# The up-products of a group: two blocks of rows in turns, one product each

## The chip, the cores and the metric

The kernel runs on one core of one Trainium2 chip. The metric is the time of one execution on the device in microseconds (us). The core has five engines that work side by side, each through its own queue in order: TensorE (PE, matrix products; PEld are its loads of the stationary operand), VectorE (DVE), ScalarE (ACT), GpSimd (POOL), and SyncE (SP), which here only issues DMAs. Products are written to PSUM, which holds few tiles; DVE and ACT read it, POOL and the DMAs do not use it here.

## The reference

The input x is (2, 4096, 256). A gated recurrence runs over the 4096 steps of each sequence, then a feed-forward part with binary weights; each has a residual and a layer norm behind it:

```python
u = x @ W_in + b_in
g = sigmoid(x @ W_gate + b_gate)
h_t = tanh(h_{t-1} @ A + u_t @ Bm)          # 64 states, step by step
y_t = g_t * (h_t @ C.T + u_t @ D.T) + (1 - g_t) * x_t
x = layernorm(x + (y @ W_out + b_out + x))
# bw = mean(|w|, axis=1) * sign(w), for w1 and w2
h = gelu(x @ bw1.T + b1)                    # 256 -> 1024
x = layernorm(x + (h @ bw2.T + b2))         # 1024 -> 256
```

All values are float32.

## The kernel before

**Chunks.** Each sequence is cut into 64 segments of 64 steps, and all 128 segments (both sequences) run side by side, so that a recurrence step is one product and one tanh on 128 columns (`steps`, L156 to 158). The 8192 tokens are worked in 16 chunks of 512. The first 85 us load data, form u and most of the gates, and run the first steps. Then a loop over the chunks c follows (L718 to 783), which interleaves pieces of several chunks, and into which `emit` strews the remaining recurrence steps: a piece is a generator, and at each of its `yield`s a counter of PE time may let one step be put in.

**A chunk's pieces.** `mix` (L365, products ps_y at L370) and `mix_end` form y with DVE's operations d (L377, L382) and tg (L385); `project` (L388, products ps_z at L395) multiplies by W_out in two halves, DVE adds the residual (L406) and gathers statistics (L256, L260, L265), POOL takes the power -1/2 (L266). `shift` (nm, L271) and `norm` (L279, four ACT operations for most chunks) apply the layer norm. `turn` (L418) transposes the result (ps_t, L423); ACT copies it to fp32r as xhi (L431), and DVE takes the rest, xlo (L433). `rest` adds a row on POOL (L355).

**The feed-forward part.** The 1024 hidden rows are 8 blocks of 128, worked in four groups g of two. `up(g)` (L442) makes, for each block, four products of 512 columns into a PSUM tile ps_h (L451): sign weights times xhi for both halves of the 256 features, then times xlo. GELU on ACT (L458) reads the tile and writes h; after both blocks ACT copies h to fp32r, hhi (L467). `low(g)` (L470) has DVE compute hlo = h - hhi (L474). `down(g)` (L532) multiplies hhi and hlo by the second sign weights, 32 products of 256 columns into ps_o (L490), 16 after each half of the group. After the fourth group `scale` (o, L506) and `add` (L512) move the sum out on DVE, and `store` norms it (L281) and stores it.

**Order.** The engines' orders are written out by hand: PE, ACT, DVE and POOL execute what the code emits, in that order. In chunk c it is: up 0, low 0, down 2 of chunk c-1, shift and norm of c+1, mix of c+2, up 1, down 3 of c-1, add and statistics of c-1, one gate (c from 1 to 12), turn of c+1, low 1, rest, up 2, low 2, store of c-1, down 0, first half of the projection of c+2, up 3, down 1, low 3, second half of the projection. A group is written c.g below: 13.0 is group 0 of chunk 13. In the first loop pass (c = 0) and for the last chunk there is less to put between: up 1 of chunk 0 follows up 0 at once, and up 2 of chunk 15 follows up 1 at once (L772 to L776). The last chunk ends with `down_end` (L544), which finishes block by block of tokens; its group 3 copies hi and subtracts lo in two halves (`apart`).

**PSUM tiles.** The pool p_1 (tag h) has three tiles of one bank, taken in turn by ps_h, ps_g and ps_u. p_m (tag m) is a single tile of two banks, taken in turn by ps_y, ps_t and ps_z. p_2 (tag o) is the single ps_o. A product that is first to write a tile waits until the last reader of the tile's earlier use is done. In SBUF h has two buffers, hhi and hlo three.

Of the kernel before, what the change touches and what calls it, by code (L numbers as in the profile page):

```python
# [8 lines left out]
FP = mybir.dt.float32  # L9
# [7 lines left out]
P = 128  # L17
B, T, DM, S, H = 2, 4096, 256, 64, 1024
KD = DM // P
# [4 lines left out]
N = 512  # L24
# [13 lines left out]
def gated_recurrence_then_binary_ffn(  # L38
# [24 lines left out]
    p_1 = ctx.enter_context(tc.tile_pool(name="p_1", bufs=3, space=PSUM))  # L63
# [15 lines left out]
    sg1 = cp.tile([P, KD, H], FR, name="sg1")  # L79
# [249 lines left out]
    class Chunk:  # L329
# [112 lines left out]
        def up(self, g, apart=False):  # L442
            nm = f"{self.nm}_{g}"
            h = wk.tile([P, 2, N], FP, tag="h", name=f"h{nm}")
            hi = wk.tile([P, 2, N], FR, tag="hhi", name=f"hhi{nm}", bufs=3)
            self.h[g] = h, hi
            for i in range(2):
                j = 2 * g + i
                ps = p_1.tile([P, N], FP, tag="h", name=f"ps_h{nm}_{i}")
                for n, (k, part) in enumerate((k, p) for p in (self.hi, self.lo) for k in range(KD)):  # L450
                    nc.tensor.matmul(  # L451
                        ps,
                        sg1[:, k, bass.ts(j, P)],
                        part[:, k, :],
                        start=n == 0,
                        stop=n == 2 * KD - 1,
                    )
                nc.scalar.activation(  # L458
                    h[:, i, :],
                    ps,  # L460
                    AF.Gelu,
                    bias=b1_c[:, j : j + 1],
                    scale=al1[:, j : j + 1],
                )
                if i == 1:
                    for part in range(2) if apart else [slice(0, 2)]:
                        nc.scalar.copy(hi[:, part, :], h[:, part, :])  # L467
                yield
# [379 lines left out]
```

## Time and profile before

| | |
|---|---|
| median of three runs | 453.91 us (452.56 to 455.10) |
| profiled execution | 452.42 us, span from first to last instruction 450.6 us |
| PE busy | 439.4 us, 98% of the span; granted clock 0.996 in the mean |
| DVE, ACT, POOL busy | 358.7, 261.2, 173.6 us |
| L451, products ps_h | 512: 256 with xhi, 256 with xlo |
| L458, GELU | 128, 776 ns each in the mean |
| L467, copy to hhi | 65, 1037 ns |
| L474, hlo | 65, 1314 ns |

How to read it: a row of the profile names the line, the engine, the operation, out<-in by the program's tile names, the shape and a count. In the rows ordered by time the first number is the start in us from the span's start, the second the time from there to the end, of several merged instructions where the count is over 1; in square brackets stands the idle time of the engine before it and what ended it. Rows of waits read: who <- whom: us in total, times, longest. An fp32 product is recorded as two instructions. The end of a matmul is modelled, so that products overlap in the records; their starts are what tells the pace. PEclk gives the granted clock of TensorE in tenths, a digit for each fortieth of the span.

### The profile page before, as it was taken

What the parts mean: (1) busy time and instruction counts of PE and PEld (TensorE: products, weight loads), DVE (VectorE), ACT (ScalarE), POOL (GpSimd) and SP (SyncE); (2) the same over time, 40 slices, a digit from 0 to 9 for tenths busy, and PEclk for the clock granted to TensorE, in tenths of its full rate; (3) what the DMA queues carried; (4) which work ended last, traced back from release to release, by engine and by line L of the source; (5) the groups of instructions that cost most, each with busy time, mean ns of one, the idle gap of its engine ahead of it and who ended that gap; (6) DMA issues with size and microseconds to landing.
All of it is one profiled execution on the core that took longest, in us unless ns stands there. A gap on an engine that the chain in (4) does not pass through costs nothing.

```text
span 450.6 us, 6727 instructions
## 1 busy us (share of the span) xinstructions
PE 439.4 (98%) x2506; PEld 357.2 (79%) x2506; DVE 358.7 (80%) x597; ACT 261.2 (58%) x424; POOL 173.6 (39%) x177
## 2 busy tenths in 40 slices
PE   9999999999999999999999999999999999999992
PEld 5665766788888888888978787979798888897982
DVE  0245937967989798989898988898998989887774
ACT  2443541585656575847574747475666656565871
POOL 1001400644545434343454454535353545433413
PEclk9999999999999999999999999999999999999998
DMA  8898824220223222322233122212111020201012
GB/s 298 306 318 289 291 64 135 69 85 0 71 95 116 96 70 95 116 95 70 95 97 112 49 71 93 73 45 72 47 51 67 13 93 1 93 1 48 1 47 99
DMA packets 14837, 44.50 MB, mean 99 GB/s; under 512 B 2000, under 2 KB 3024, under 8 KB 14800
## 3 DMA queue, kind: packets, MB, share of 16 engines
q1 hardware_dynamic: 14224, 43.65, 28.8%
q8 instruction: 21, 0.34, 0.3%
q10 hardware_dynamic: 576, 0.37, 0.3%
q14 instruction: 16, 0.13, 0.1%
HBM read 31.43 MB, written 8.39 MB: 88 GB/s over the span
## 4 chain that ended last, share of the span: by engine, by line
PE 88%; DVE 6%; ACT 2%; DMA 2%; POOL 1%; issue 0%; POOLq 0%; DVEq 0%
PE ps_h L451 24%; PE ps_o L490 23%; PE ps_z L395 12%; PE ps_g L313 11%; PE ps_y L370 6%; PE ps_s L157 5%; PE ps_u L131 4%; PE ps_t L423 3%; DVE hlo L474 1%; DMA xt<-in_xT 1%; ACT xn L279 1%; DVE xn L281 1%; PE ps_s L154 1%; ACT h L458 1%; DVE bs_a L256 1%; ACT hhi L467 1%
## 5 line engine op out<-in xcount | busy, mean ns | idle before, releaser
L458 ACT ACTIVATE h<-ps_h,bias_c,al 128x512 f32<-128x512 f32 x128 | 97.5, 776 | 77.4 <-PE ps_h L451 72.2
L490 PE MATMUL ps_o<-sg,hhi 128*128 128x256 f32 x496 | 120.3, 282 | 0.0
L490 PE MATMUL ps_o<-sg,hlo 128*128 128x256 f32 x496 | 119.0, 279 | 0.1
L474 DVE TENSOR_TENSOR hlo<-h,hhi 128x1024 fp32r<-128x1024 f32 (+1 forms) x65 | 84.2, 1314 | 23.6 <-ACT hhi L467 23.6
L490 PEld LDWEIGHTS ps_o<-sg,hhi 128*128 128x128 f32 x496 | 93.6, 189 | 2.3
L490 PEld LDWEIGHTS ps_o<-sg,hlo 128*128 128x128 f32 x496 | 93.4, 188 | 2.5 <-DVE hlo L474 0.3
L451 PE MATMUL ps_h<-xhi,sg 128*128 128x512 f32 x256 | 92.3, 441 | 0.0
L451 PE MATMUL ps_h<-xlo,sg 128*128 128x512 f32 x256 | 80.2, 394 | 0.2
L355 POOL TENSOR_TENSOR xn<-xn,bo_r 128x256 f32<-128x256 f32 x64 | 60.7, 979 | 45.5 <-DMA xn<-in_x 45.5
L355 POOL TENSOR_TENSOR xn<-xn,b_r 128x256 f32<-128x256 f32 x64 | 71.5, 1145 | 1.2 <-PE ps_t L423 1.2
L467 ACT CAST hhi<-h 128x1024 fp32r<-128x1024 f32 (+1 forms) x65 | 67.3, 1037 | 2.0
L313 PE MATMUL ps_g<-xt,w_gate 128*128 128x384 f32 (+3 forms) x208 | 67.1, 432 | 0.2 <-DMA xt<-in_xT 0.2
L266 POOL TENSOR_TENSOR rs_a<-rs_a,neg_half 128x4 f32<-128x4 f32 x16 | 17.2, 1075 | 122.3 <-DVE rs_a L265 104.6
L158 ACT ACTIVATE st<-ps_s 64x128 f32<-64x128 f32 x112 | 30.1, 269 | 56.2 <-PE ps_s L157 55.8
L395 PE MATMUL ps_z<-w_out,tg 128*128 128x256 f32 x256 | 61.2, 380 | 0.0
L451 PEld LDWEIGHTS ps_h<-xlo,sg 128*128 128x128 f32 x256 | 48.1, 188 | 11.9 <-DVE xlo L433 0.9
L451 PEld LDWEIGHTS ps_h<-xhi,sg 128*128 128x128 f32 x256 | 46.1, 189 | 12.8 <-issue 6.2
L266 POOL TENSOR_TENSOR rs_b<-rs_b,neg_half 128x4 f32<-128x4 f32 (+1 forms) x17 | 19.2, 1132 | 95.5 <-DVE rs_b L265 84.3
L157 PEld LDWEIGHTS ps_s<-st,wab 128*128 128x128 f32 x224 | 37.5, 189 | 22.8 <-ACT st L158 9.5
L395 PEld LDWEIGHTS ps_z<-w_out,tg 128*128 128x128 f32 x256 | 45.9, 190 | 5.0
L279 ACT ACTIVATE xn<-xn,nm_a,rs_a 128x256 f32<-128x256 f32 x60 | 31.2, 591 | 26.5 <-DVE nm_a L271 26.5
L157 PE MATMUL ps_s<-st,wab 128*128 128x128 f32 x224 | 43.9, 277 | 0.0
(73 smaller groups left out, 485.3 us busy)
## 6 DMA issues: line engine op xcount, KB each, us to landing
xt<-in_xT SPq DMA_DIRECT2D x35, 512.0 KB, 4.6
xn<-in_x SPq DMA_DIRECT2D x16, 512.0 KB, 3.5
out_y<-xn SPq DMA_DIRECT2D x15, 512.0 KB, 2.6
hu<-st SPq DMA_DIRECT2D x32, 128.0 KB, 2.9
w1t<-in_w1T SPq DMA_DIRECT2D x2, 512.0 KB, 5.7
w1n<-in_w SPq DMA_DIRECT2D x2, 512.0 KB, 6.6
w2t<-in_w2T SPq DMA_DIRECT2D x2, 512.0 KB, 4.7
xt<-in_xT SPq DMA_DIRECT2D x2, 256.0 KB, 3.5
```

The costliest lines, as they stand in the source:

```text
L157: nc.tensor.matmul(p_h, ab, st[:, j].rearrange("p b k -> p (b k)"), start=True, stop=True)
L158: nc.scalar.activation(h_of[:, j + 1].rearrange("p b k -> p (b k)"), p_h[TOP, :], AF.Tanh)
L266: nc.gpsimd.tensor_tensor(rs, rs, neg_half[:, cut], ALU.pow)
L279: nc.scalar.activation(r, r, AF.Identity, bias=self.sh[:, i : i + 1], scale=rs)
L313: nc.tensor.matmul(ps[:, cut], w_gate[:, k, bass.ts(m, P)], xt_[:, k, cut], start=k == 0 and i == 0, stop=k == KD - 1, skip_group_check=True,)
L355: nc.gpsimd.tensor_tensor(r[:, i, :], r[:, i, :], row, ALU.add)
L395: nc.tensor.matmul(self.ps_z[:, i, :], self.y[:, k, bass.ts(i, P)], w_out[:, k, :], start=k == 0, stop=k == KD - 1,)
L451: nc.tensor.matmul(ps, sg1[:, k, bass.ts(j, P)], part[:, k, :], start=n == 0, stop=n == 2 * KD - 1,)
L458: nc.scalar.activation(h[:, i, :], ps, AF.Gelu, bias=b1_c[:, j : j + 1], scale=al1[:, j : j + 1],)
L467: nc.scalar.copy(hi[:, part, :], h[:, part, :])
L474: nc.vector.tensor_sub(lo[:, i, :], h[:, i, :], hi[:, i, :].bitcast(FP))
L490: nc.tensor.matmul(ps[:, i, :], part[:, j % 2, bass.ts(tb, P)], sg2[:, j, :], start=j == 0 and part is self.h[j // 2][0] and first, stop=j ...
```

## The change

Only `up` is changed. Both PSUM tiles are taken at its start. The loop over the four products (feature half and part) is now the outer one, and the loop over the two blocks the inner one, so that the products go: first product of block 0, first of block 1, second of block 0, and so on. The two GELUs, the copy after the second one and the two `yield`s follow behind all eight products. `low`, `down` and the order of the pieces stay as they were.

```diff
-            for i in range(2):
-                j = 2 * g + i
-                ps = p_1.tile([P, N], FP, tag="h", name=f"ps_h{nm}_{i}")
-                for n, (k, part) in enumerate((k, p) for p in (self.hi, self.lo) for k in range(KD)):
+            both = [p_1.tile([P, N], FP, tag="h", name=f"ps_h{nm}_{i}") for i in range(2)]
+            for n, (k, part) in enumerate((k, p) for p in (self.hi, self.lo) for k in range(KD)):
+                for i in range(2):
                     nc.tensor.matmul(
-                        ps,
-                        sg1[:, k, bass.ts(j, P)],
+                        both[i],
+                        sg1[:, k, bass.ts(2 * g + i, P)],
                         part[:, k, :],
                         start=n == 0,
                         stop=n == 2 * KD - 1,
                     )
+            for i in range(2):
+                j = 2 * g + i
                 nc.scalar.activation(
                     h[:, i, :],
-                    ps,
+                    both[i],
                     AF.Gelu,
                     bias=b1_c[:, j : j + 1],
                     scale=al1[:, j : j + 1],
```

## The prediction

> **What bounds the kernel now.** I read the page's busy shares first, then its slices, the waits, and last the order of time in one chunk.
>
> ```profile
> PE 439.4 (98%) x2506; PEld 357.2 (79%) x2506; DVE 358.7 (80%) x597; ACT 261.2 (58%) x424; POOL 173.6 (39%) x177
> ...
> PEclk9999999999999999999999999999999999999998
> ```
>
> TensorE (PE) is busy in every slice until the last and its clock is full. Between 97 and 413 us its start times show hardly a hole. So time can be won only by quicker products, and lost wherever PE starts to wait. The waits say how near it is to that:
>
> ```profile
> ACT h L458 <- PE ps_h L451: 72.2, 40, 2.8
> ...
> DVE hlo L474 <- ACT hhi L467: 23.6, 29, 3.5
> ...
> PEld ps_h L451 <- DVE xlo L433: 0.9, 2, 0.5
> ...
> PE ps_t L423 <- ACT xn L279: 0.9, 4, 0.4
> ```
>
> ScalarE (ACT) waits 40 times for up-products, VectorE (DVE) waits 29 times for ACT's hi copy. PE's matmuls themselves wait only under 1 us a line once the chunks run. One chunk shows the loop that runs through all three:
>
> ```profile
> 222.81 1.69 ACT L458 ACTIVATE h<-ps_h,bias_c,al 128x512 f32<-128x512 f32 x2 [0.66 <-PE ps_h L451]
> ...
> 224.53 1.05 ACT L467 CAST hhi<-h 128x1024 fp32r<-128x1024 f32 x1
> ...
> 225.61 1.23 DVE L474 TENSOR_TENSOR hlo<-h,hhi 128x1024 fp32r<-128x1024 f32 x1 [0.81 <-ACT hhi L467]
> ...
> 231.53 1.21 DVE L506 TENSOR_TENSOR o<-ps_o,al_r 128x1024 f32<-128x1024 f32 x1
> ...
> 235.83 1.22 DVE L433 TENSOR_TENSOR xlo<-ps_t,xhi 128x1024 fp32r<-128x1024 f32 x1
> ...
> 237.46 1.60 PEld L395 LDWEIGHTS ps_z<-w_out,tg 128*128 128x128 f32 x8
> ```
>
> Products of group 0 end, GELU twice, hi copy, and DVE, which stood idle 0.81 us for that copy, starts hlo. From there DVE works its queue without a hole (nm, d twice, tg, o, xn, statistics) until xlo ends at 237.05. xlo is the last reader of the single p_m tile, and the projection that takes this tile loads its first weights at 237.46. That is 0.41 us, or 0.36 after the 0.05 us a release takes (in chunk 0 xlo ended at 96.65 and PE's load started at 96.70). What comes later than 0.36 us stops PE.
>
> **The change part by part.**
>
> *Instructions.* None is added or removed: 512 products with 512 weight loads, 128 GELUs, 65 hi copies and as many lo subtractions. No DMA and no SP or POOL instruction is moved. A recurrence step that fell between the two blocks of a group now comes behind all eight products; its two small products cost the same 0.22 us there.
>
> *Pace of the products.* They now change bank at each product, not once in four. In the trace the step from product 4 to 5 of a group is that bank change: 231 ns from start to start, beside 230 to 233 ns for the other steps. So 0, with bounds of ±3 ns × 512 = ±1.5 us. [...] The fp32 projection products do run at 216 here, these do not. [...] But this trace holds four idles within 413.1 to 415.3 us, PE busy only 3.11 of 4.00 us, and a granted clock of 1.00 there; the idles expected below are shorter. So 0.
>
> *GELU and what follows.* Block 0 used to end after product 4, so that its GELU ran under products 5 to 8. Now it ends with product 7. The two ways stand in the trace: where ACT waited for products (the first line), the pair takes 1.69 us; where both blocks were ready, it takes less:
>
> ```profile
> 418.40 1.45 ACT L458 ACTIVATE h<-ps_h,bias_c,al 128x512 f32<-128x512 f32 x2
> 419.88 1.05 ACT L467 CAST hhi<-h 128x1024 fp32r<-128x1024 f32 x1
> ```
>
> A GELU starts 0.44 us after the start of its last product (429.81 to 430.25 below). Before, the copy starts 0.44 + 0.81 us after the start of product 8. Now the first GELU starts 0.44 us after product 7 starts, the copy 1.48 us later (418.40 to 419.88), and product 8 starts 0.23 us after product 7: 0.44 + 1.48 − 0.23 = 1.69 against 1.25. So the hi copy is late by 0.44 us wherever ACT stood idle for the group. Groups 1 are excepted: their GELUs wait for the norm anyway.
>
> *Where that lands.* The direct consumers, the down products, have hlo 2.7 us or more ahead of need from chunk 1 to 13: no cost. But hlo of group 0 starts DVE's unbroken run, and behind it queue nm (so the norm on ACT), d, tg, o, xn, the statistics and xlo, for which the projection's load waits. In half of the chunks d itself waits some 0.1 us for ps_y (once 0.57), which absorbs as much. The room before the load, read as above for projections 3 to 14, is 0.27, 0.51, 0.33, 0.28, 0.14, 0.36, 0.27, 0.47, 0.33, 0.28, 0.15 and 0.00 us; the lateness that reaches xlo is 0.44, 0.39, 0.35, 0.33, 0.33, 0.44, 0.44, 0, 0.36, 0.33, 0.33, 0.44. What exceeds the room is 0.17 + 0 + 0.02 + 0.05 + 0.19 + 0.08 + 0.17 + 0 + 0.03 + 0.05 + 0.18 + 0.44 = **1.38 us**. PE's stall moves the next group too, so it recurs in each chunk. Bounds: 0, if DVE makes it good, and 3.7 us, if in about half of the chunks one DVE operation more falls under POOL traffic (L385 takes 1.65 us instead of 1.22 beside POOL's additions), which removes the room.
>
> *The norm of the last chunk.* From hlo of 13.0 at 388.90 to the norm at 413.10 DVE, ACT and POOL form one chain, and the transposes wait for that norm (the 0.9 us of the waits). Late by 0.44: **+0.44 us**; 0 to 0.9.
>
> *First group.* Up 0 of chunk 0 waits for the low half of x before products 3 and 4 (0.9 us of holes), with four hi products now ahead of it: it ends at 89.19 instead of 89.98, −0.79. But up 1 follows at once, and here the third buffer matters: a group's second tile is the previous group's first. Up 1 needs it at its second product (89.42), while its GELU, started at 89.16, frees it at about 89.90: +0.48. Its late copy of x for projection 2 costs another 0.04. Together **−0.27 us**; −0.8 to +0.2.
>
> *Last chunk.* Up 2 follows up 1 at once, too:
>
> ```profile
> 430.25 0.78 ACT L458 ACTIVATE h<-ps_h,bias_c,al 128x512 f32<-128x512 f32 x1 [2.85 <-PE ps_h L451]
> 431.19 0.78 ACT L458 ACTIVATE h<-ps_h,bias_c,al 128x512 f32<-128x512 f32 x1 [0.15 <-PE ps_h L451]
> ```
>
> Up 1 runs 429.12 to 430.98. Its first GELU now starts at 430.95, frees its tile at about 431.70, and product 2 of up 2 wanted it at 431.21: +0.5. Then group 3's copies are late by 0.44, and PE already waits 0.24 us at 439.39 for the second hlo half: +0.44. Nothing behind covers it. **+0.94 us**; 0.5 to 1.4. Elsewhere at least a down group, a projection or the transposes lie between two up groups, longer than the two GELUs.
>
> *Sum.* −0.27 + 1.38 + 0.44 + 0.94 = +2.49 us, or 0.55%. The profiled execution took 452.42 us (span 450.6, 1.8 around it): 454.9. The median of the runs, 453.91, lies 1.5 us above it: 456.4. I say **456.5 us**.
>
> **The rivals.** *DVE makes it good.* ACT is 58% busy and DVE waits 29 times, so lateness may vanish before xlo. Only first group, norm and tail remain: +1.1, 455.0. Against it: no hole stands between hlo and xlo in most chunks.
>
> *DVE loses more.* In the stretches of 25 us from 200 to 400 us it is busy for 21.8 to 23.1 us. With the 3.7 us for the chunks the sum is +4.8: 458.7. For it: room is 0.15 us or less three times; against it: POOL's additions start before hlo's wait and do not move.
>
> *Faster: the products quicken.* If the 15 ns above the fp32 pace come from accumulating four times running into one bank, alternation wins up to 7.7 us: 453.91 − 7.7 + 2.5 = 448.7. It decides from 5 ns per product on (2.49 us / 512). Against it stands the 231 ns of the bank change.
>
> *It does nothing*: the compiled order keeps the written order of PE and ACT, so I give this no chance of its own.
>
> **How the numbers follow.** The likeliest case gets 0.55, with its own range 455.2 to 458.5; DVE makes it good 0.13; DVE loses more 0.20; faster 0.12. About 0.5% is what a measurement of this kernel can tell from no change: 451.6 to 456.2. Of the likeliest, two thirds lie above: slower 0.37 + 0.20 = 0.57, same 0.18 + 0.13 = 0.31, faster 0.12. The range 453.4 to 460 leaves out the faster case and a few hundredths above.
>
> **What would show it.** GELU pairs of 1.45 us instead of 1.69, and about as many hi copies waited for by DVE, with more time in all than 23.6 us; a new wait of PE's loads of ps_z for xlo of 1 to 2 us; a wait of ps_h for a GELU at the first group and near 431 us; the wait for xlo at L451 gone; PE's starts for ps_h still 225 to 235 ns apart. I am wrong if these starts fall below 226 ns, if ps_z waits nowhere, or if the clock shows less than full.

## The result and the profile after

The changed kernel takes 455.47 us in the median of 12 runs, the kernel before, run beside it, 452.93 us. The medians are 2.5 us apart. The ratio worked out from the runs is 1.0064, with a 95% interval from 1.0048 to 1.0081: slower by 2.9 us, somewhere between 2.2 and 3.7. The profiled execution took 454.76 us, its span is 453.0 us against 450.6. The page shows that neither the work nor the clock has changed:

```profile
PE 439.9 (97%) x2506; PEld 357.0 (79%) x2506; DVE 357.3 (79%) x597; ACT 256.3 (57%) x424; POOL 181.8 (40%) x177
...
PEclk9999999999999999999999999999999999999998
```

PE has as many instructions and as much busy time as before (439.4 us), so the 2.4 us of the span are waiting. The same chunk as in the prediction, in order of time:

```profile
223.70 1.45 ACT L459 ACTIVATE h<-ps_h,bias_c,al 128x512 f32<-128x512 f32 x2 [1.35 <-PE ps_h L450]
225.18 1.05 ACT L468 CAST hhi<-h 128x1024 fp32r<-128x1024 f32 x1
226.26 1.69 DVE L475 TENSOR_TENSOR hlo<-h,hhi 128x1024 fp32r<-128x1024 f32 x1 [1.26 <-ACT hhi L468]
...
236.52 1.22 DVE L433 TENSOR_TENSOR xlo<-ps_t,xhi 128x1024 fp32r<-128x1024 f32 x1
...
237.79 1.38 PEld L395 LDWEIGHTS ps_z<-w_out,tg 128*128 128x128 f32 x7
```

ACT waits twice as long for the group (1.35 us instead of 0.66), then works both GELUs in 1.45 us instead of 1.69. DVE waits 1.26 us for the hi copy instead of 0.81. xlo ends at 237.74, and the projection's load starts 0.05 us behind it: the 0.36 us of room are used up. The waits of the whole kernel (who <- whom: us, times, longest):

```profile
DVE hlo L475 <- ACT hhi L468: 33.5, 30, 3.8
...
PEld ps_h L450 <- ACT h L459: 1.7, 2, 0.8
...
PEld ps_h L450 <- ACT tg L361: 0.9, 1, 0.9
...
PE ps_t L423 <- ACT xn L279: 1.3, 4, 0.8
...
PEld ps_z L395 <- DVE xlo L433: 0.5, 1, 0.5
```

The wait of ps_h for xlo is gone. New are the waits of ps_h for GELUs and for a tanh, and the wait of ps_z for xlo; the wait of the last transposes grew by 0.4 us (0.9 before).

Both traces hold the same products in the same order of pieces, so the start of a piece in one trace less its start in the other tells how far PE has fallen behind, and each stage's loss is the growth of that lag. (Before the first up group the lag differs from trace to trace, from -0.9 to +3.1 us, with the arrival of the data and, in the +3.1 of "only groups 0", with a granted clock of 0.91 in the mean from 72 to 90 us; it is no part of the change and is left out. In the changed kernel's trace it is -0.62 us, which is why its span grew by only 2.4.) Rows add up to the growth of the lag within 0.15 us. In us:

| stage | predicted | after | only groups 0 | only chunks 0 and 15 | A B AAA BBB | AAA BBB A B |
|---|---|---|---|---|---|---|
| first two groups | -0.27 | +0.64 | -0.05 | +0.63 | +0.24 | +0.03 |
| ps_z, projections 3 to 14 | +1.38 | +0.82 | +0.87 | 0.00 | +0.09 | +1.00 |
| last norm, transposes | +0.44 | +0.40 | +0.42 | 0.00 | 0.00 | +0.42 |
| chunk 15, group 2 | +0.5 | +0.66 | -0.07 | +0.6 | +0.05 | +0.1 |
| behind group 3 of chunk 15 | +0.44 | +0.44 | +0.04 | +0.44 | 0.0 | +0.46 |
| sum | +2.49 | +2.96 | +1.2 | +1.7 | +0.4 | +2.0 |

The other columns are the experiments below; A and B stand for a product of block 0 and of block 1.

### The profile page after: what moved, and what is told of

It is laid out like the page before. It is cut to its first block, busy times and chain, and to the rows that moved or that the text cites. A ratio compares the mean times of both kernels' runs of the same rounds, so it can differ in the third digit from the quotient of the medians.

```text
span 453.0 us, 6727 instructions
## 1 busy us (share of the span) xinstructions
PE 439.9 (97%) x2506; PEld 357.0 (79%) x2506; DVE 357.3 (79%) x597; ACT 256.3 (57%) x424; POOL 181.8 (40%) x177
## 4 chain that ended last, share of the span: by engine, by line
PE 88%; DVE 5%; ACT 2%; DMA 2%; POOL 1%; issue 1%; SPq 0%; POOLq 0%; DVEq 0%
PE ps_h L450 24%; PE ps_o L491 23%; PE ps_z L395 12%; PE ps_g L313 11%; PE ps_s L157 6%; PE ps_y L370 6%; PE ps_u L131 3%; PE ps_t L423 3%; DMA xt<-in_xT 1%; ACT h L459 1%; DVE hlo L475 1%; DVE xn L281 1%; POOL rs_b L266 1%; DVE bs_b L256 1%; DMA hu<-st 0%
## 5 line engine op out<-in xcount | busy, mean ns | idle before, releaser
L459 ACT ACTIVATE h<-ps_h,bias_c,al 128x512 f32<-128x512 f32 x128 | 93.2, 773 | 92.8 <-PE ps_h L450 89.9
L355 POOL TENSOR_TENSOR xn<-xn,bo_r 128x256 f32<-128x256 f32 x64 | 69.6, 1118 | 45.3 <-DMA xn<-in_x 45.3
L450 PE MATMUL ps_h<-xhi,sg 128*128 128x512 f32 x256 | 82.4, 441 | 1.4 <-ACT h L459 0.8
L355 POOL TENSOR_TENSOR xn<-xn,b_r 128x256 f32<-128x256 f32 x64 | 70.8, 1136 | 2.0 <-PE ps_t L423 2.0
L450 PE MATMUL ps_h<-xlo,sg 128*128 128x512 f32 x256 | 69.0, 391 | 0.0
```

What stands on the lines that cost most here:

```text
L355: nc.gpsimd.tensor_tensor(r[:, i, :], r[:, i, :], row, ALU.add)
L450: nc.tensor.matmul(both[i], sg1[:, k, bass.ts(2 * g + i, P)], part[:, k, :], start=n == 0, stop=n == 2 * KD - 1,)
L459: nc.scalar.activation(h[:, i, :], both[i], AF.Gelu, bias=b1_c[:, j : j + 1], scale=al1[:, j : j + 1],)
```

## The experiments

**Where the loss is made.** Three kernels take the change apart by place. In `up` the new order is taken only where a condition holds, otherwise the old one:

```diff
+            if g == 0 and self.nm not in ("0", "15"):    # first kernel
+            if g > 0 and self.nm not in ("0", "15"):     # second kernel
+            if self.nm in ("0", "15"):                   # third kernel
```

> Only group 0 of chunks 1 to 14 is worked in turns; all other groups as before. Theory (lateness of group 0 runs through VectorE's unbroken queue to xlo and to the last norm): +0.8 us at the ps_z loads (most of it at projections 3, 9 and 14) and +0.4 us at the transposes of chunk 15, +1.2 us in all, ratio 1.0027. Rival (every group worked in turns costs alike): 14 of 64 groups, +0.6 us, with no new ps_z wait. Rival (the products' pace): starts of ps_h differ from 225 to 235 ns in these groups.

> Only groups 1, 2 and 3 of chunks 1 to 14 are worked in turns. Theory: their late copies have room everywhere, 0 us within 0.3 us, ratio 1.000. Rival (every group costs alike): 42 of 64 groups, +1.9 us, ratio 1.004.

> Only the groups of chunks 0 and 15 are worked in turns. Theory: +0.6 us at the first two groups (the second PSUM tile is waited for at the second product, from a tanh and from a GELU), +0.66 us at group 2 of chunk 15 (its second tile, from a GELU) and +0.44 us behind group 3 of chunk 15 (late hlo): +1.7 us, ratio 1.0038, and no wait of ps_z beyond that of before. Rival (every group costs alike): 8 of 64 groups, +0.4 us.

Measured: groups 0 alone 1.0045 (1.0024 to 1.0066), groups 1 to 3 alone 0.9993 (0.9973 to 1.0014), chunks 0 and 15 alone 1.0049 (1.0031 to 1.0066). Fourteen of the 64 groups carry a loss and 42 carry none. The traces give +1.2 and +1.7 us for the first and the third (table), inside the intervals (1.1 to 3.0 and 1.4 to 3.0 us). The first measured 2.0 us, more than the 1.2 of its trace. The clock can account for it: 11 of its 22 runs have a mean granted clock of 0.992 or less, against 5 of the 59 runs of the kernel before (see the last section). Without these runs the medians of the three kernels lie 1.25, 0.0 and 1.8 us above that of the kernel before, 452.49 us, and 3.0 us together. With groups 1 to 3 in turns, no wait of ps_z appears and the last transposes wait as before (first line); with groups 0 in turns both are those of the changed kernel (the other three):

```profile
PE ps_t L423 <- ACT xn L279: 0.9, 4, 0.4
```

```profile
PE ps_t L423 <- ACT xn L279: 1.3, 4, 0.8
...
PEld ps_z L395 <- DVE xlo L433: 0.5, 1, 0.5
PE ps_z L395 <- DVE xlo L433: 0.3, 1, 0.3
```

The rival that every group worked in turns costs alike is out.

**The end of block 0, or the alternation.** Two other orders of the same eight products, in all groups:

```diff
-            for n, (k, part) in enumerate((k, p) for p in (self.hi, self.lo) for k in range(KD)):
-                for i in range(2):
+            each = [(k, p) for p in (self.hi, self.lo) for k in range(KD)]
+            for i, n in ((0, 0), (1, 0), (0, 1), (0, 2), (0, 3), (1, 1), (1, 2), (1, 3)):   # A B AAA BBB
+            for i, n in ((0, 0), (0, 1), (0, 2), (1, 0), (1, 1), (1, 2), (0, 3), (1, 3)):   # AAA BBB A B
```

> All groups, but in another order of the same eight products: block 0 once, block 1 once, block 0 three times, block 1 three times. The second tile is still taken at the second product and three bank changes lie in a group, but block 0 ends with product 5, early enough for its GELU to be over when block 1 ends. Theory: the copy to hhi is not late (0 to 0.05 us), so nothing at ps_z, at the last norm and behind the last group; the tile wait of group 2 of chunk 15 falls to under 0.1 us, that of group 1 of chunk 0 by about half; left is the wait for the tanh in the first group: +0.3 us, ratio 1.0007, from -0.2 to +0.7 us. Rival (two open tiles or bank changes cost in themselves): between before and after by the share of bank changes, 2 more against 6 more, +1.0 us or above.

> All groups in a third order: block 0 three times, block 1 three times, block 0, block 1. Block 0 ends with product 7 as in the changed kernel, but the second tile is taken at the fourth product and there are three bank changes. Theory: lateness as in the changed kernel, +0.8 us at ps_z, +0.4 us at the last transposes, +0.44 us behind the last group; tile waits shrink to 0.2 us in the first two groups and 0.05 us at group 2 of chunk 15: +2.0 us in all, ratio 1.0044. Rival (bank changes cost): 2 changes more than before, where the changed kernel has 6, a third of its loss, +1.0 us, and the ps_z waits shrink in the same measure.

Measured: A B AAA BBB 0.9997 (0.9976 to 1.0018), AAA BBB A B 1.0055 (1.0032 to 1.0077). The two have equally many bank changes, and nearly the whole loss lies between them. In the first, the hi copy starts 1.24 us after the start of product 8, as before the change, in all groups 0 but two that have a recurrence step beside them, and ps_z and the last transposes show no more than 0.1 us of loss, although the second tile is open from the second product on. In the second it starts 1.68 us after it, as in the changed kernel, and both losses are back. So it is the late end of block 0 that costs, not the turns. The first two groups show the opposite picture: here the order that takes its second tile at the second product loses (0.24), the one that takes it at the fourth does not (0.03). (The profiled execution of the second lost another 1.55 us to the clock, which the table leaves out and the last section tells.)

**The lateness by itself.** The kernel before, with its own order of products; ACT only gets one or two idle copies before the hi copy of group 0 in chunks 1 to 14:

```diff
                 if i == 1:
+                    if g == 0 and self.nm not in ("0", "15", "s"):
+                        nc.scalar.copy(idle, h[:, 0, :192])       # both kernels
+                        nc.scalar.copy(idle, h[:, 0, 192:384])    # the second kernel only
                     for part in range(2) if apart else [slice(0, 2)]:
                         nc.scalar.copy(hi[:, part, :], h[:, part, :])
```

> The kernel before with its own product order everywhere; only, in group 0 of chunks 1 to 14, ACT makes one idle copy of 192 columns between the second GELU and the copy to hhi, some 0.44 us. Theory (lateness alone is the cause, the order of the products is not): the same loss at the same places as with only these groups in turns, +0.8 us at the ps_z loads, half of it at projection 14, and +0.4 us at the transposes of chunk 15: +1.2 us, ratio 1.0027. Rival (the open tiles and their order cost the time): 0 us.

> As the run with one idle copy, with two, some 0.87 us of lateness. Theory (each chunk loses what the lateness exceeds the room before the ps_z load, read from the changed kernel's trace): +5.3 us at the ps_z loads, now in every chunk, 0.3 to 0.85 us each, and +0.85 us at the last transposes: +6.2 us, ratio 1.0136, that is five times the loss for twice the lateness. Rival (loss in proportion to the lateness): +2.5 us.

Measured: 1.000 (0.9978 to 1.0021) and 1.0037 (1.0019 to 1.0056). Both expectations were wrong in the dose. The idle copy lies partly under the end of the GELU before it, as ACT's rows in the second kernel show:

```profile
222.39 1.69 ACT L459 ACTIVATE h<-ps_h,bias_c,al 128x512 f32<-128x512 f32 x2 [0.66 <-PE ps_h L452]
223.98 0.34 ACT L467 COPY idle<-h 128x192 f32<-128x192 f32 x1
224.36 0.35 ACT L468 COPY idle<-h 128x192 f32<-128x192 f32 x1
224.62 1.04 ACT L471 CAST hhi<-h 128x1024 fp32r<-128x1024 f32 x1
```

The hi copy starts 1.74 us after the start of product 8 with two copies, 1.35 with one, 1.24 without. The doses were 0.50 and 0.11 us, not 0.87 and 0.44. Read with these, the two runs still answer the question: 0.11 us cost 0.10 us at ps_z (all of it at projection 14, which had no room) and 0.04 at the transposes; 0.50 us cost 1.33 and 0.46. Between them lies the changed kernel with 0.44, 0.82 and 0.40. Lateness alone, with the old order of products, makes the loss at both places. And the loss does not grow in proportion: of 0.50 us, the end of xlo moves by 0.41, 0.45, 0.21, 0.23, 0.23, 0.48, 0.63, 0.42, 0.21, 0.24, 0.21 and 0.48 us against product 8 for projections 3 to 14; less the rooms of the prediction, and counted as zero where that is negative, this makes 0.14 + 0.09 + 0.12 + 0.36 + 0.06 + 0.48 = 1.25 us, against 1.33 measured.

**The last norm.** The four DVE operations of 3.1 us that norm chunk 12 (L281) stand in the queue before the norm of chunk 15. They were moved to ACT, first in place, then behind group 3 of chunk 13, in the kernel before and in the changed one:

```diff
             else:
-                do(c - 1, "store")
+                do(c - 1, "store", range(TB), nc.scalar if c == end - 2 else nc.vector)   # in place
...
-            else:
+            elif c != end - 2:                                                           # behind
                 do(c - 1, "store")
...
             do(c, "low", 3)
-            if c == end - 1:
-                do(c - 1, "store")
+            if c >= end - 2:                                                             # behind
+                do(c - 1, "store", range(TB), nc.scalar if c == end - 2 else nc.vector)
```

> The kernel before; only the norm of chunk 12 ahead of its store, four DVE operations of 3.1 us in the last stretch before the norm of chunk 15, goes to ACT, which stands idle there. Theory (the norm of the last chunk hangs on DVE's unbroken queue, so that PE waits 1.4 us at its transposes): DVE reaches that norm more than 1 us earlier, the transposes wait no longer, -1.4 us, ratio 0.997. Rival (the norm hangs on ACT or on POOL): no change.

> The changed kernel with the same move of the norm of chunk 12 to ACT. Theory: the wait at the last transposes goes, the 0.4 us that the change added there included: 1.8 us below the changed kernel; against the kernel before +2.96 - 1.8 = +1.1 us, ratio 1.0025. The 0.8 us at ps_z, the 0.6 us of the first group and the 1.1 us of the last chunk stay. Rival (lateness moves to the next wait): the time of the changed kernel, 1.0064.

Measured: 1.0058 (1.0036 to 1.0079) and, in 5 runs, 1.0137 (1.0107 to 1.0166): the first slower instead of faster, the second far slower than the 1.0025 expected. ACT in the first of the two kernels:

```profile
405.39 2.08 ACT L279 ACTIVATE xn<-xn,nm_b,rs_b 128x256 f32<-128x256 f32 x4 [5.51 <-DVE nm_b L271]
407.38 1.43 ACT L458 ACTIVATE h<-ps_h,bias_c,al 128x512 f32<-128x512 f32 x2
```

The norm on ACT waits for DVE's nm, nm for POOL, and the GELUs of the group behind it in ACT's queue start at 407.38 instead of some 402.5 (401.50 in the kernel before, and this trace runs 1.0 us late); the queue in front of the last norm had become ACT's. Of the 3.3 us that PE falls behind in this profile, 1.5 belong to the clock (last section). With the product order of the change it is worse, since PE wants the first GELU's tile at its second product: it waited 1.36 us there against 0.27. Moved behind that group:

> The kernel before; the norm of chunk 12 goes to ACT, but behind the GELUs and the lo part of group 3 of chunk 13, so that it holds no GELU of that group up, as it did when it stood before them. Theory (the last norm hangs on DVE's queue, 3.1 us of which are taken out): its wait at the transposes of chunk 15 falls from 1.4 us to 0.5 us or less, the GELUs of 14.0 come 0.8 us later without harm: -1.0 us, ratio 0.998. Rival (what is late on ACT costs as much as DVE wins): no change.

> The changed kernel with the same move. Theory: the wait at the last transposes, 1.8 us in the changed kernel, falls to about 0.9 us, since the GELUs of 14.0 are 0.4 us later still; the other losses stay: +2.0 us against the kernel before, ratio 1.0044. Rival: 1.0064 as the changed kernel.

Measured: 0.9998 (0.998 to 1.0015) and 1.0057 (1.0036 to 1.0078). DVE does reach the statistics of chunk 15 at 407.99 instead of 409.54, but then waits for a hi copy that the norm on ACT made late, and the norm starts at 412.73 instead of 413.10:

```profile
411.39 1.23 DVE L474 TENSOR_TENSOR hlo<-h,hhi 128x1024 fp32r<-128x1024 f32 x1 [1.08 <-ACT hhi L467]
```

PE's lag falls by 0.47 us at the transposes with the order before, and with the change it stays where it was instead of growing by 0.40: the difference between the two orders stays, as the theory of lateness has it, but the 1 us expected is not won. No kernel here is measurably faster than the one before.

## Why the prediction was right, point by point

- *Sign and size.* +2.49 us predicted, +2.9 measured (+2.96 by the stages). The likeliest case held. But two terms were wrong in opposite directions, by +0.9 and -0.6 us, and that they nearly cancelled was luck. The 456.5 us named came out 1.0 us high, because the sum started from 453.91 us, and the same kernel took 452.93 in the runs beside the change.
- *Instructions and pace.* Right. The steps between starts of ps_h within a block of products are 225 to 237 ns, before and after, and 230.7 ns before and 230.5 after in the mean. The faster rival needed 5 ns per product and there were none. Its yardstick was loose, too: the 216 ns of the projection belong to fp32 instructions of 256 columns, not of 512, so that they say nothing of what a product for ps_h could reach.
- *GELU and what follows.* Right: the hi copy starts 1.68 us after product 8 against 1.24, 0.44 us later. Groups 1, which wait for the norm, and groups 2 and 3 cost nothing (second experiment).
- *ps_z.* The mechanism was right, the size was not: 0.82 us for 1.38. The term that was mis-sized is what DVE's wait for ps_y absorbs. I had read it as some 0.1 us from the wait's own figure. In six chunks the run from hlo to the end of xlo takes 11.70 us before and 11.45 after, so 0.25 us were absorbed. DVE in chunk 5, before and after:

```profile
203.17 0.69 DVE L271 SCALAR_TENSOR_TENSOR nm_a<-mv_a,rs_a 128x4 f32<-128x4 f32 x1
203.97 1.23 DVE L377 TENSOR_TENSOR d<-ps_y,xt 128x1024 f32<-128x1024 f32 x1
205.23 1.81 DVE L382 SCALAR_TENSOR_TENSOR d<-tg,d 128x1024 f32<-128x1024 f32 x1
207.07 1.23 DVE L385 SCALAR_TENSOR_TENSOR tg<-xt,d 128x1024 f32<-128x1024 f32 x1
```

```profile
203.79 0.69 DVE L271 SCALAR_TENSOR_TENSOR nm_a<-mv_a,rs_a 128x4 f32<-128x4 f32 x1
204.40 1.21 DVE L377 TENSOR_TENSOR d<-ps_y,xt 128x1024 f32<-128x1024 f32 x1
205.65 1.31 DVE L382 SCALAR_TENSOR_TENSOR d<-tg,d 128x1024 f32<-128x1024 f32 x1
```

Without a wait d starts 0.61 us behind nm, before nm's record ends; with the wait of 0.11 us it starts 0.80 us behind it. So the wait had cost 0.19 us, not 0.11. The two operations after d, one of which runs longer, beside POOL's additions, take 1.81 + 1.23 us before and 1.31 + 1.65 us after, some 0.1 us less. In the six, lateness then stays within the room or exceeds it by 0.04 us at most. What remains is 0.15, 0.07, 0.17 and 0.41 us at projections 3, 8, 9 and 14, and 0.03 elsewhere. (The view of the waits shows only 0.5 + 0.3 us at ps_z, below the 1 to 2 us expected of it.) DVE losing more, the heavier rival, did not come: from 95 us on, 25 of the operations d, tg and hlo take 1.64 us or more before and 25 after, all of them beside POOL's additions of L355, but not the same ones (in the chunk of the first section hlo takes 1.69 us instead of 1.23, and L385 1.23 instead of 1.66).
- *The last norm.* Right: 0.40 us for 0.44.
- *First group.* Wrong by 0.9 us, +0.64 for -0.27, and in its sign: the one step of the prediction whose mechanism failed. It did see that a group's second tile is another's, and looked only at up 1. Up 0 takes at its second product a tile that a tanh of a gate was still reading, which the old order did not want before the fifth. PE in the changed kernel (its waits in brackets):

```profile
86.73 0.48 PE L450 MATMUL ps_h<-xhi,sg 128*128 128x512 f32 x1
87.75 0.96 PE L450 MATMUL ps_h<-xhi,sg 128*128 128x512 f32 x3 [0.54 <-ACT tg L361]
88.55 1.08 PE L450 MATMUL ps_h<-xlo,sg 128*128 128x512 f32 x4
89.47 0.40 PE L450 MATMUL ps_h<-xhi,sg 128*128 128x512 f32 x1
90.27 0.97 PE L450 MATMUL ps_h<-xhi,sg 128*128 128x512 f32 x3 [0.41 <-ACT h L459]
```

The tanh was in the trace of before, where it ended at 88.32, while up 0 had begun at 87.34:

```profile
87.63 0.69 ACT L361 ACTIVATE tg<-ps_g,bg_c 128x512 f32<-128x512 f32 x1
```

The saved wait for xlo is real (the four lo products follow one another), but the tanh's wait takes its place.

- *Last chunk.* Right in both parts: 0.66 us for 0.5, since the load of the weights, which started 0.23 us ahead of the product for block 0 (432.01 and 432.24), waits too (0.84 us), and 0.44 for 0.44. The tile's wait reads

```profile
432.24 0.39 PE L450 MATMUL ps_h<-xhi,sg 128*128 128x512 f32 x1
433.04 0.97 PE L450 MATMUL ps_h<-xhi,sg 128*128 128x512 f32 x3 [0.41 <-ACT h L459]
```

- *The clock.* Full throughout the chunks in the profile of the changed kernel, as taken. The ground given for it was weak: the idles expected were not all shorter than those of the trace, since +0.44 us at the last transposes makes 0.8 us of the 0.4 that stood there. And in the profile of AAA BBB A B the clock fell behind idles of 0.81 and three times 0.16 us; see the last section.

## What to carry to other kernels

Work done in turns ends together: each consumer but the last loses its head start, and the end of the last one's chain moves too if one engine serves both. Before doing so, look for the consumer that runs an unbroken queue behind that chain, and compare the lateness, here 0.44 us, with the room at the far end of that queue, chunk by chunk: only what exceeds it costs, but it costs again in each round. And a buffer that is taken sooner has to be free sooner: ask for each first use who read that buffer last, also where another kind of work used it.

## What the runs showed of the hardware

Behind an idle of some 0.8 us and three of 0.16 us the granted clock of PE fell in one profile and stayed full in another. In the profiled execution of AAA BBB A B PE waited 0.81 us and then three times 0.16 us at the last transposes, the last of these until 417.40. From 416 us on the granted clock is 0.96, 0.50 and 0.69 in the mean of three stretches of 2 us, and 1.00 ahead of them and behind them (stretches; after the stretch: its length, busy us of PE, PEld, DVE, ACT and POOL with instruction counts, PEclk, DMA share, GB/s):

```profile
412.00:416.00 4.00, 3.19 (x23) 2.78 (x21) 3.93 (x14) 0.73 (x2) 1.02 (x1) 1.00 0.01 2
416.00:418.00 2.00, 1.51 (x9) 0.94 (x9) 0.37 (x1) 2.00 (x5) 1.48 (x1) 0.96 0.00 0
418.00:420.00 2.00, 2.00 (x7) 1.61 (x6) 0.00 (x0) 1.97 (x4) 2.00 (x3) 0.50 0.00 0
420.00:422.00 2.00, 2.00 (x10) 1.66 (x9) 1.30 (x2) 1.29 (x2) 1.67 (x3) 0.69 0.00 0
422.00:424.00 2.00, 2.00 (x16) 1.88 (x15) 1.12 (x2) 1.87 (x3) 0.00 (x0) 1.00 0.00 0
```

The eight products for ps_h that begin at 418.00 take 3.43 us from the first start to that of the product behind them; in the trace of before they take 1.93 us (from 415.75). The lower clock cost 1.55 us of lag on top of the 2.0 us of the table. The same was seen in the profile with the norm of chunk 12 moved in place (1.56 and three times 0.16 us of waiting, 1.48 us of lag, a mean clock of 0.989). In the changed kernel's profile the waits were 0.79 and three times 0.16 us, as long, and the clock stayed at 1.00 in each stretch of 2 us from 414 to 424 us. So the length of the idles alone does not tell whether the clock falls. What else decides, these traces do not show.

How often the clock fell outside the profiles can be estimated from each run's mean clock. These two profiled executions have a mean of 0.992 and 0.989. Groups 0 alone, with 0.992, shows 0.91 in the mean from 72 to 90 us, behind a wait of 2.4 us for a DMA (the changed kernel waits 0.7 us there and shows 1.00). The changed kernel with the norm in place has 0.992, the other nine profiles have 0.993 or more. If 0.992 or less is taken as the sign, the clock fell in 14 of the 149 runs of the kernel before that have a clock on record, and in 9 of the 91 of the six kernels that wait at most 0.5 us for the first of the last transposes. It fell in 37 of the 79 runs of five kernels that wait 0.8 us or more there: groups 0 alone (11 of 22), two idle copies (8 of 20), AAA BBB A B (6 of 16) and the norm in place (9 of 16 and 3 of 5). The changed kernel waits as long, and shows it in 1 of 12. Where in those runs the clock fell is not on record, so that lateness brings such falls on is likely, but not shown. The prediction had taken this cost as nothing, from idles that left the clock full in one trace.
